# Moving a step's exponential behind its value products in a masked attention layer

## The chip, the cores and the metric

The kernel runs on one core of one Trainium2 chip. The metric is the device time of one execution in microseconds, taken as the median of several runs. A core has five engines that work side by side, each through its own queue of instructions in program order: TensorE (PE in the profile; its weight loads are shown apart as PEld), VectorE (DVE), ScalarE (ACT), GpSimd (POOL) and SyncE (SP, which here only issues transfers). They wait for each other through semaphores. TensorE's products land in PSUM, which the program divides into eight banks.

## The reference, cut to what matters

One graph-attention layer with a residual: x is 8 frames of 2048 rows by 256 channels, adj a 2048 x 2048 mask that all frames share, 8 heads of 32 channels.

```python
qkv = jnp.einsum('fnc,ck->fnk', x, w_qkv)
q, k, v = jnp.split(qkv, 3, axis=-1)
# ... reshaped to (F, N, H, D), H = 8, D = 32
scores = jnp.einsum('fnhd,fmhd->fhnm', q, k) / jnp.sqrt(jnp.asarray(D, x.dtype))
mask = (adj > 0)[None, None, :, :]
scores = jnp.where(mask, scores, jnp.asarray(-1000000000.0, x.dtype))
attn = jax.nn.softmax(scores, axis=-1)
t = jnp.einsum('fhnm,fmhd->fnhd', attn, v).reshape(F, N, C)
x = _layernorm(x + t, ln1_g, ln1_b)
h = jax.nn.relu(jnp.einsum('fnc,cd->fnd', x, w1) + b1)
f_out = jnp.einsum('fnd,dc->fnc', h, w2) + b2
x = _layernorm(x + f_out, ln2_g, ln2_b)
# ... and around the layer: x = _layernorm(x_in + layer(x_in))
```

## The kernel before

The attention is cut into **items** (f, qc, g, mb): frame f, a chunk qc of 512 queries, a group g of four heads, and a block mb of 128 keys. There are 8 x 4 x 2 x 16 = 1024 items. The sixteen items with the same (f, qc, g) form a **group**; there are 64 groups. One item is one **step** of the main loop.

A step computes the scores of the item two ahead (LEAD = 2), and the value products of its own item. `scores` makes four products, one for each head, into two PSUM pairs; VectorE adds the mask to them and writes them to SBUF, and ScalarE takes the exponential of all 128 x 2048 elements in place.

```python
def scores(item):
    f, qc, g, mb = item
    pt = PT[item] = pp.tile([P, 4, CH], F32, name="p")     # pp has 10 buffers
    ps2 = [score_pair() for _ in range(2)]                 # 3 pairs of banks, in turn

    for half in (1, 0):
        for j in range(2):
            r = D * (2 * half + j)
            nc.tensor.matmul(ps2[half][:, j, :], KT[...][r:r + D, ...],
                             QT[f, qc, g][r:r + D, :], start=True, stop=True)
    for half, ps in enumerate(ps2):
        nc.vector.tensor_tensor(pt[:, 2 * half:2 * half + 2, :], ps,
                                MK[f, qc][:, mb, None, :].to_broadcast([P, 2, CH]), ALU.add)
    nc.scalar.activation(pt, pt, AF.Exp, scale=1.0 / math.sqrt(D))

LAST = MB - 1

def values(item):
    f, qc, g, mb = item
    grp = (f, qc, g)
    if mb == 0:
        i = state["side"]
        O[grp] = ps_x[i].tile([P, CH], F32, name=f"x{i}")
    for h in range(4):
        r = D * h
        nc.tensor.matmul(O[grp][r:r + D, :], V[...][:, mb % TPC, r:r + D], PT[item][:, h, :],
                         start=(mb == 0), stop=(mb == LAST))
    if mb == LAST:
        OT[grp] = op.tile([P, CH], F32, name=f"oT{g}")
        nc.scalar.copy(OT[grp], O.pop(grp))
```

Six of the eight PSUM banks serve the scores. The two others, ps_x, change roles from group to group: one gathers the value products of the running group, and the other is the only bank for everything else (projections, transposes, the layer's dense part), which is called **fill** here. At a group's end the roles are swapped, so the bank that fill gets next is the one that the finished group's values are still in, until ScalarE has copied them out to oT.

```python
def bank(dt=F32):
    shape = [P, CH] if dt == F32 else [P, 2, CH]
    if state["side"] is not None:
        i = 1 - state["side"]
        return ps_x[i].tile(shape, dt, name=f"x{i}")
    # ... (only the opening, before the main loop)

def channels(pool, name, xT, k0):          # fill: queries and keys
    ps = bank()
    for a in range(2):
        nc.tensor.matmul(ps, wqkv[:, a, k0:k0 + P], xT[:, a, :], start=(a == 0), stop=(a == 1))
    t = pool.tile([P, CH], F32, name=name)
    nc.scalar.copy(t, ps)
    return t
# project(): channels() for the keys, then the values' projection, each after a "yield BANK"
# tail(), second dense product, fill too:
for jj in range(0, TPC, 2):
    yield BANK
    ps = bank()
    for j in range(jj, jj + 2):
        for d in range(2):
            nc.tensor.matmul(ps[:, (j - jj) * C:(j - jj + 1) * C], hT[:, d, j * P:(j + 1) * P], w2s[:, d, :], ...)
    nc.vector.tensor_tensor(z[:, jj:jj + 2, :], ps.rearrange(...), z[:, jj:jj + 2, :], ALU.add)
```

The main loop puts at most one piece of fill (`advance(t, 1)`) ahead of a step's scores, and none in a group's first step:

```python
for t, (f, qc, g, mb) in enumerate(items):
    if mb == 0 and t:
        state["side"] = 1 - state["side"]
    # ... (what fill is to start)
    if mb:
        advance(t, 1)
    if t + LEAD < len(items):
        # ... (brings a projection forward if its V is still missing)
        scores(items[t + LEAD])
    values(items[t])
    add_up(items[t])          # sums for the denominators: GpSimd adds and adding transfers
    if mb == LAST:
        start(t + SUM, denominator(f, qc, g), t)
```

Of the kernel before, what the change touches and what calls it, by code (L numbers as in the profile page):

```python
# [14 lines left out]
AF = mybir.ActivationFunctionType  # L15
# [5 lines left out]
D = 32  # L21
# [32 lines left out]
def fast_path(ctx, tc, cst, x, adj, out, RS):  # L54
    nc = tc.nc
# [24 lines left out]
    def score_pair():  # L80
        i = state["pair"]
        state["pair"] = (i + 1) % 3
        return ps_s[i].tile([P, 2, CH], F32, name=f"s{i}")
# [45 lines left out]
    def mask_blocks(qc, mc, cv):  # L129
        for half in range(2):  # L130
            yield BANK
            ps = bank(BF16)
            for r in range(2):
                for j in range(TPC):
                    rr = 2 * half + r
                    nc.tensor.transpose(ps[:, r, j * P:(j + 1) * P], cv[:, j, rr * P:(rr + 1) * P], identb)
            nc.vector.tensor_tensor(MK[0, qc][:, mc * TPC + 2 * half:mc * TPC + 2 * half + 2, :], ps,
                                    cst["ones"][:, 0:1, None].to_broadcast([P, 2, CH]), ALU.min, saturate=False)
        if mc == NCK - 1:
            nc.sync.dma_start(MD[qc], words(MK[0, qc]))  # L140

    def load_mask(f, qc):
        MK[f, qc] = mkp.tile([P, MB, CH], F8, name="mask")
        nc.sync.dma_start(words(MK[f, qc]), MD[qc])
# [5 lines left out]
    def queries(f, c, xT):  # L150
        for g in range(2):
            yield BANK
            QT[f, c, g] = channels(qp, "qT", xT, g * P)

    def turn_rows(xc, xT):
# [3 lines that stand above are left out]
            for j in range(TPC):  # L159
                nc.tensor.transpose(ps[:, j * P:(j + 1) * P], xc[:, j, a * P:(a + 1) * P], ident)  # L160
            nc.scalar.copy(xT[:, a, :], ps)
# [32 lines left out]
    def project(f, c, g, xT=None):  # L194
        if xT is None:
            xT = yield from reload(f, c)
            while len(KT) < (2 * f + g) * NCK + c:
                yield 1
        yield BANK
        KT[f, c, g] = channels(kp, "kT", xT, C + g * P)  # L200
        yield BANK
        ps = bank()
        for j in range(TPC):
            for a in range(2):
                nc.tensor.matmul(ps[:, j * P:(j + 1) * P], xT[:, a, j * P:(j + 1) * P],  # L205
                                 wqkv[:, a, 2 * C + g * P:2 * C + (g + 1) * P], start=(a == 0), stop=(a == 1))
        v = vp.tile([P, TPC, P], F32, name="v")
        nc.scalar.copy(v, ps.rearrange("p (j c) -> p j c", c=P))
        V[f, c, g] = v
        give(xT)  # L210


    PT, O, OT, RC = {}, {}, {}, {}

    def scores(item):
        f, qc, g, mb = item
        pt = PT[item] = pp.tile([P, 4, CH], F32, name="p")
        ps2 = [score_pair() for _ in range(2)]
# [4 lines that stand above are left out]
                nc.tensor.matmul(ps2[half][:, j, :], KT[f, mb // TPC, g][r:r + D, (mb % TPC) * P:(mb % TPC + 1) * P],  # L223
                                 QT[f, qc, g][r:r + D, :], start=True, stop=True)
        for half, ps in enumerate(ps2):
            nc.vector.tensor_tensor(pt[:, 2 * half:2 * half + 2, :], ps,  # L226
                                    MK[f, qc][:, mb, None, :].to_broadcast([P, 2, CH]), ALU.add)
        nc.scalar.activation(pt, pt, AF.Exp, scale=1.0 / math.sqrt(D))  # L228

    LAST = MB - 1  # L230

# [8 lines that stand above are left out]
            nc.tensor.matmul(O[grp][r:r + D, :], V[f, mb // TPC, g][:, mb % TPC, r:r + D], PT[item][:, h, :],  # L240
# [4 lines that stand above are left out]
# [8 lines left out]
    def add_up(item):  # L253
        f, qc, g, mb = item
        for chain in MOVED:
            if mb in chain[1:]:
                nc.gpsimd.dma_start(PT[f, qc, g, chain[0]], PT.pop(item), accum_op=ALU.add)  # L257
        if mb in POOLED[1:]:
            first = PT[f, qc, g, POOLED[0]]
            nc.gpsimd.tensor_tensor(first, first, PT.pop(item), ALU.add)  # L260
# [119 lines left out]
    def start(t, gen, due):  # L380
        fill.append([t, gen, 1, due])
        fill.sort(key=lambda e: e[3])
# [24 lines left out]
    def mask_ahead(qc):  # L407
        for mc in range(NCK):
            yield from turn_mask(qc, mc)

    items = [(f, qc, g, mb) for f in range(F) for qc in range(NCK) for g in range(2) for mb in range(MB)]
    LEAD = 2
# [6 lines left out]
    def begin():  # L419
        flat = [pp.tile([P, 4, CH], F32, name="p").rearrange("p a q -> p (a q)") for _ in range(NCK + NCK // 2)]  # L420
        cols = [t.bitcast(I32).rearrange("p (j m) -> p j m", m=CH) for t in flat[:NCK]]
        cv = [t[:, i * 2 * CH:(i + 1) * 2 * CH].bitcast(BF16).rearrange("p (j m) -> p j m", m=CH)
              for t in flat[NCK:] for i in range(2)]
        rows = [pp.tile([P, 4, CH], F32, name="p") for _ in range(NCK)]
        for c in range(NCK):
            xc = rows[c][:, 0:2, :].rearrange("p a (b c) -> p (a b) c", c=C)
            nc.sync.dma_start(xc, x[0, c * CH:(c + 1) * CH, :].rearrange("(j p) c -> p j c", p=P))
            nc.sync.dma_start(cols[c], adj[0:CH, c * CH:(c + 1) * CH].rearrange("(j p) m -> p j m", p=P))
        MK[0, 0] = mkp.tile([P, MB, CH], F8, name="mask")
        for c in range(NCK):  # L430
            nc.vector.tensor_scalar(cv[c], cols[c], 0.0, MASKED, op0=ALU.is_le, op1=ALU.mult)
            xT = rows[c][:, 2:4, :]
            yield from turn_rows(rows[c][:, 0:2, :].rearrange("p a (b c) -> p (a b) c", c=C), xT)
            nc.sync.dma_start(XD[0][c], xT)
            XT[0, c] = xT
            if c == 0:
                yield from queries(0, 0, xT)
            yield from project(0, c, 0, xT)
            yield from mask_blocks(0, c, cv[c])
        for k in range(LEAD):  # L440
            scores(items[k])
        for c in range(NCK):
            yield from project(0, c, 1, rows[c][:, 2:4, :])

# [5 lines left out]
    for _ in begin():  # L450
        pass
# [3 lines left out]
# [3 lines that stand above are left out]
        if f == 0 and g == 0 and mb == 0 and qc + 1 < NCK:  # L458
            start(t, mask_ahead(qc + 1), t + 28)
        if g == 1 and mb == 0 and (f or qc == NCK - 1) and (f + 1 < F or qc + 1 < NCK):  # L460
            load_mask(f + (qc + 1) // NCK, (qc + 1) % NCK)
        if f + 1 < F:
            for what, *which in NEXT.get((2 * qc + g, mb), []):
                due = t + MB // 2 if what is turn else items.index((f + 1, 0, which[1], which[0] * TPC)) - LEAD - 1
                start(t, what(f + 1, *which), due)
# [3 lines that stand above are left out]
            nf, _, ng, nmb = items[t + LEAD]  # L469
            t0 = t  # L470
            while (nf, nmb // TPC, ng) not in V:
                advance(t0, 1)
                t0 += 1
            scores(items[t + LEAD])
        values(items[t])
        add_up(items[t])
        if mb == LAST:
            start(t + SUM, denominator(f, qc, g), t)
    t = len(items)
# [128 lines left out]
def kernel(  # L608
# [56 lines left out]
    nc.gpsimd.memset(RS[:, 1], 1.0)  # L665

    fast_path(tc, cst, x, adj, out, RS)


# [49 lines left out]
```

## Time and profile before

| | |
|---|---|
| median of three runs | 3736.42 us (3731.55 to 3740.82) |
| profiled execution: span | 3732.1 us |
| mean granted TensorE clock | 0.977 |
| groups of 16 steps | 64, most of them 48 to 64 us from one copy of the values to the next |

The profile is read from top to bottom: first the busy time of each engine over the whole span, then the groups of instructions by source line, each with its total busy time, the mean duration of one, and the idle time of its engine just before it together with what ended that idle time. A short name such as "L244" is line 244 of the kernel before: L223 the score products, L226 the mask's addition, L228 the exponential, L240 the value products, L244 the copy of a group's values, L180 and L205 projections, L352 and L362 the two dense products, L136 the transposes of the mask in the first frame, L294 the denominators. The timeline lists instructions in order of their start; equal neighbours are merged, and one product shows as two records.

### The profile page before, as it was taken

How to read it: one execution, taken by the hardware profiler on the slowest of the kernel's cores; microseconds unless marked ns; L12 is line 12 of the kernel's file. 1: busy time of each engine (PE TensorE's matmuls, PEld its weight loads, DVE VectorE, ACT ScalarE, POOL GpSimd, SP SyncE). 2: the span in 40 equal slices, each digit the busy share in tenths (PEclk: the TensorE clock that was granted, in tenths of full speed). 3: DMA queues.
4: the chain of work that ended last, by engine and by line, in shares of the span. 5: the costliest groups of instructions: out<-in, count | busy, mean ns of one | idle time of the engine just before them, and what ended most of it. 6: DMA issues, size and time to landing. Idle time of an engine off the chain costs nothing. (4 is left out here: it accounts for less than half of the span.)

```text
span 3732.1 us, 53786 instructions
## 1 busy us (share of the span) xinstructions
PE 3241.8 (87%) x22020; PEld 1038.8 (28%) x22020; DVE 2760.8 (74%) x3203; ACT 2411.0 (65%) x1921; POOL 2599.1 (70%) x1363
## 2 busy tenths in 40 slices
PE   7877888899988899889998899889898889988884
PEld 4222223222322233222332223222232222322221
DVE  4777766877688766788677777777768877688883
ACT  3554555766667666766666776666666676677663
POOL 2555666777677775877667785777777777687775
PEclk9998999999999999999999999999999999999997
DMA  6766675776766775776766776676676676676664
GB/s 185 175 142 152 146 175 117 168 162 142 173 150 145 158 171 145 169 153 154 169 138 151 163 172 158 140 165 154 147 175 141 148 171 152 154 164 140 139 134 86
DMA packets 113774, 573.31 MB, mean 154 GB/s; under 512 B 10833, under 2 KB 27729, under 8 KB 60273
## 3 DMA queue, kind: packets, MB, share of 16 engines
q0 software_dynamic: 64848, 436.90, 58.1%
q1 hardware_dynamic: 47856, 131.61, 10.0%
q8 instruction: 174, 2.85, 0.3%
q10 hardware_dynamic: 816, 1.31, 0.1%
q14 instruction: 80, 0.65, 0.0%
HBM read 129.37 MB, written 37.75 MB: 45 GB/s over the span
## 5 line engine op out<-in xcount | busy, mean ns | idle before, releaser
L226 DVE TENSOR_TENSOR p<-s,mask 128x1024 f32<-128x1024 f32 x2048 | 2410.3, 1219 | 753.8 <-PE s L223 480.0
L228 ACT ACTIVATE p<-p 128x2048 f32<-128x2048 f32 x1024 | 1957.1, 1911 | 1232.9 <-DVE p L226 916.2
L260 POOL TENSOR_TENSOR p<-p 128x2048 f32<-128x2048 f32 x384 | 1835.9, 4810 | 653.6 <-ACT p L228 645.0
L223 PE MATMUL s<-qT,kT 32*128 32x512 f32 x8192 | 1193.2, 652 | 232.5 <-DVE p L226 231.0
L240 PE MATMUL x<-p,v 128*32 128x512 f32 x8192 | 1112.2, 616 | 0.0
L257 POOL DMA_DIRECT2D p<-p x384 | 382.7, 1018 | 351.2 <-ACT p L228 138.9
L223 PEld LDWEIGHTS s<-qT,kT 32*128 32x128 f32 x8192 | 325.3, 186 | 853.6 <-DVE p L226 695.6
L240 PEld LDWEIGHTS x<-p,v 128*32 128x32 f32 x8192 | 162.3, 108 | 795.2 <-issue 645.1
L180 PE MATMUL x<-in,wqkv 128*128 128x512 f32 x472 | 234.6, 620 | 23.1 <-ACT oT L244 10.2
L278 ACT ACTIVATE y<-y,nb,rs 128x256 f32<-128x256 f32 x384 | 224.9, 589 | 38.0 <-POOL nb L275 38.0
L294 PE MATMUL x<-p,ones 128*32 128x512 f32 x2048 | 246.3, 599 | 1.8 <-DVE y L364 0.9
L267 DVE BATCH_NORM_STATS2 st<-y 128x6 f32<-128x256 f32 x384 | 160.1, 417 | 27.1 <-DMA y<-in_x_dram 27.1
L362 PE MATMUL x<-w2s,hT 128*128 128x256 f32 x512 | 127.6, 392 | 45.7 <-ACT oT L244 42.3
L352 PE MATMUL x<-turned,w1s 128*128 128x512 f32 x256 | 128.8, 626 | 20.8 <-ACT hT L353 19.5
L180 PEld LDWEIGHTS x<-in,wqkv 128*128 128x128 f32 x472 | 80.3, 190 | 186.1 <-issue 69.8
L362 PEld LDWEIGHTS x<-w2s,hT 128*128 128x128 f32 x512 | 92.1, 190 | 112.0 <-ACT oT L244 68.6
L205 PE MATMUL x<-wqkv,in 128*128 128x128 f32 x896 | 114.9, 282 | 6.4 <-ACT kT L182 6.3
L205 PEld LDWEIGHTS x<-wqkv,in 128*128 128x128 f32 x896 | 104.2, 192 | 55.0 <-ACT kT L182 34.0
L364 DVE TENSOR_TENSOR y<-x,y 128x512 f32<-128x512 f32 x64 | 44.3, 692 | 94.9 <-PE x L362 94.7
L294 PEld LDWEIGHTS x<-p,ones 128*32 128x32 f32 x2048 | 64.0, 111 | 165.8 <-issue 129.7
L272 POOL TENSOR_TENSOR rs<-rs,mhalf 128x4 f32<-128x4 f32 x96 | 99.3, 1035 | 8.0
L341 PE MATMUL x<-ident,y 128*128 128x128 f32 x256 | 48.0, 299 | 54.5 <-ACT turned L342 38.8
(87 smaller groups left out, 1427.1 us busy)
## 6 DMA issues: line engine op xcount, KB each, us to landing
p<-p POOLq DMA_DIRECT2D x384, 1024.0 KB, 9.7
y<-in_x_dram POOLq DMA_DIRECT2D x64, 512.0 KB, 6.1
in<-xd SPq DMA_DIRECT2D x59, 512.0 KB, 8.0
mask<-md SPq DMA_DIRECT2D x28, 1024.0 KB, 6.6
out_dram<-y SPq DMA_DIRECT2D x32, 512.0 KB, 3.0
in<-in_x_dram SPq DMA_DIRECT2D x28, 512.0 KB, 6.9
xd<-in SPq DMA_DIRECT2D x28, 512.0 KB, 10.0
in<-in_adj_dram SPq DMA_DIRECT2D x24, 512.0 KB, 7.6
```

The source lines that it names most:

```text
L180: nc.tensor.matmul(ps, wqkv[:, a, k0:k0 + P], xT[:, a, :], start=(a == 0), stop=(a == 1))
L205: nc.tensor.matmul(ps[:, j * P:(j + 1) * P], xT[:, a, j * P:(j + 1) * P], wqkv[:, a, 2 * C + g * P:2 * C + (g + 1) * P], start=(a == 0), s ...
L223: nc.tensor.matmul(ps2[half][:, j, :], KT[f, mb // TPC, g][r:r + D, (mb % TPC) * P:(mb % TPC + 1) * P], QT[f, qc, g][r:r + D, :], start=Tr ...
L226: nc.vector.tensor_tensor(pt[:, 2 * half:2 * half + 2, :], ps, MK[f, qc][:, mb, None, :].to_broadcast([P, 2, CH]), ALU.add)
L228: nc.scalar.activation(pt, pt, AF.Exp, scale=1.0 / math.sqrt(D))
L240: nc.tensor.matmul(O[grp][r:r + D, :], V[f, mb // TPC, g][:, mb % TPC, r:r + D], PT[item][:, h, :], start=(mb == 0), stop=(mb == LAST))
L257: nc.gpsimd.dma_start(PT[f, qc, g, chain[0]], PT.pop(item), accum_op=ALU.add)
L260: nc.gpsimd.tensor_tensor(first, first, PT.pop(item), ALU.add)
L267: nc.vector.bn_stats(st, t[:, j, :])
L278: nc.scalar.activation(t[:, j, :], t[:, j, :], AF.Identity, bias=nb[:, j:j + 1], scale=rs[:, j:j + 1])
L294: nc.tensor.matmul(ps[r:r + D, :], cst["ones"], term[:, h, :], start=(n == 0), stop=(n == 3))
L362: nc.tensor.matmul(ps[:, (j - jj) * C:(j - jj + 1) * C], hT[:, d, j * P:(j + 1) * P], w2s[:, d, :], start=(d == 0), stop=(d == 1))
```

## The change

The exponential is taken out of `scores` and put behind `values` in the loop. In ScalarE's queue this alters the order in one place only: in a group's last step, the copy of the group's values now stands ahead of the exponential of the item two ahead, where it stood behind it. In the fifteen other steps `values` gives ScalarE nothing, so the queue is as it was. No instruction is added or taken away. The purpose is to hand the bank of a finished group to fill earlier.

```diff
@@ scores()
         for half, ps in enumerate(ps2):
             nc.vector.tensor_tensor(pt[:, 2 * half:2 * half + 2, :], ps,
                                     MK[f, qc][:, mb, None, :].to_broadcast([P, 2, CH]), ALU.add)
-        nc.scalar.activation(pt, pt, AF.Exp, scale=1.0 / math.sqrt(D))
+
+    def exponentials(item):
+        nc.scalar.activation(PT[item], PT[item], AF.Exp, scale=1.0 / math.sqrt(D))
@@ the opening, before the main loop
         for k in range(LEAD):
             scores(items[k])
+            exponentials(items[k])
@@ the main loop
             scores(items[t + LEAD])
         values(items[t])
+
+        if t + LEAD < len(items):
+            exponentials(items[t + LEAD])
         add_up(items[t])
         if mb == LAST:
             start(t + SUM, denominator(f, qc, g), t)
```

## The prediction

> **What bounds the kernel now.** I read the busy shares first, then the groups by line, then the copy L244 by its tile, then one group's end in the timeline. The page's first part:
>
> ```profile
> PE 3241.8 (87%) x22020; PEld 1038.8 (28%) x22020; DVE 2760.8 (74%) x3203; ACT 2411.0 (65%) x1921; POOL 2599.1 (70%) x1363
> ```
>
> TensorE is the fullest engine, but this is an average over two kinds of steps. Steps with a piece of fill take about 4 us and are paced by TensorE; steps without take about 2.5 us and are paced by VectorE, whose two mask additions need 2 x 1219 ns. So TensorE's idle time is worth looking at by its cause. Groups of TensorE's and ScalarE's instructions (busy, mean ns of one, then idle before and its releasers):
>
> ```profile
> L223 PE MATMUL s<-qT,kT 32*128 32x512 f32 x8192 | 1193.2, 652 | 232.5 <-DVE p L226 231.0
> ...
> L180 PE MATMUL x<-in,wqkv 128*128 128x512 f32 x472 | 234.6, 620 | 23.1 <-ACT oT L244 10.2 <-ACT turned L342 6.0 <-ACT qT L182 3.3
> ...
> L362 PE MATMUL x<-w2s,hT 128*128 128x256 f32 x512 | 127.6, 392 | 45.7 <-ACT oT L244 42.3 <-ACT hT L353 2.0 <-DVE y L364 0.9
> ...
> L136 PE MATMUL x<-identb,in 128*128 128x128 bf16 x192 | 16.2, 233 | 6.1 <-ACT oT L244 4.5 <-ACT hT L353 1.4
> ```
>
> Apart from the scores' wait for VectorE, the copy L244 is the largest single cause of idle time on TensorE. The answer for the tile oT gives the number of these waits:
>
> ```profile
> L244 ACT COPY oT<-x x64: 565/567/585, 123.2 to 3664.1; 128x512 f32<-128x512 f32 x64
> ...
>   PEld x L362: 68.6, 29
>   PE x L362: 42.3, 29
>   PEld x L180: 16.6, 7
>   PEld x L240: 13.2, 16
>   PE x L180: 10.2, 7
>   PE x L136: 4.5, 3
> ```
>
> 29 + 7 + 3 = 39 of the 64 group ends make TensorE wait for the copy, 42.3 + 10.2 + 4.5 = 57.0 us in all, 1.46 us at a time. The 25 others have no fill in the group's second step, so nobody asks for the bank. One of the 39 in the timeline (start, duration, then the instruction, idle before it in brackets):
>
> ```profile
> 1917.91 1.91 ACT L228 ACTIVATE p<-p 128x2048 f32<-128x2048 f32 x1 [1.55 <-issue]
> ...
> 1919.40 1.07 PE L240 MATMUL x<-p,v 128*32 128x512 f32 x8
> 1919.60 2.36 DVE L226 TENSOR_TENSOR p<-s,mask 128x1024 f32<-128x1024 f32 x2 [0.40 <-PE s L223]
> ...
> 1921.95 1.07 PE L240 MATMUL x<-p,v 128*32 128x512 f32 x8
> 1922.04 1.91 ACT L228 ACTIVATE p<-p 128x2048 f32<-128x2048 f32 x1 [2.22 <-DVE p L226]
> 1922.16 2.35 DVE L226 TENSOR_TENSOR p<-s,mask 128x1024 f32<-128x1024 f32 x2 [0.20 <-PE s L223]
> 1923.85 0.57 ACT L244 COPY oT<-x 128x512 f32<-128x512 f32 x1
> ...
> 1924.47 1.99 PE L362 MATMUL x<-w2s,hT 128*128 128x256 f32 x8 [1.46 <-ACT oT L244]
> 1924.88 1.91 ACT L228 ACTIVATE p<-p 128x2048 f32<-128x2048 f32 x1 [0.46 <-DVE p L226]
> ```
>
> The group's last value products end at 1919.40 + 1.07 = 1920.47. ScalarE has been idle since 1917.91 + 1.91 = 1919.82, but next in its queue is an exponential, whose scores VectorE finishes at 1921.96. So the copy, ready at 1920.5, starts at 1923.85 and ends at 1924.42. TensorE, done with the next item's values at 1923.02, starts the fill product at 1924.47.
>
> **What the Trainium skill says.** The page Perfetto Trace Analysis, section Tensor Engine Instruction, says that ScalarE, VectorE and GpSimd take their instructions strictly in order, while TensorE may pull a weight load ahead of products in flight. The trace agrees: the copy stood 3.4 us behind a waiting exponential; and weight loads overlap products (PEld 28% beside PE 87%), so I count only the waits of PE and not those of PEld. The page ScalarE: Activation LUTs, section What ACT_TABLE_LOAD costs, gives 186 ns + 0.833 ns an element for immediate scale and bias: 1892 ns for 2048 elements and 612 ns for 512, with successive ones overlapping by some 93 ns. The trace has 1911 and 567 ns, and an overlap of 1923.95 - 1923.85 = 0.10 us; I use the trace's. The page TensorE: Matmul & The Clock Gate, section HAM oscillation, warns of idle gaps above about 3.4 us, which cost TensorE its clock. 1.46 us is below that, and the trace shows no penalty: the L362 product after the wait took 1.99 us, and the one in the last step before it, which followed value products without a wait, also 1.99. So I add no gain from a better clock.
>
> **The change part by part.** Removed and added: no instruction, on any engine. Moved: in 64 of 1024 steps, the copy goes ahead of one exponential.
>
> *The copy.* It can start when the last value products are done, about 1920.52 in the example, and ends 0.57 us later at 1921.09. The bank is needed at 1923.02, so there are 1.9 us to spare and the whole wait of 1.46 us goes. The other 38 waits are the same to within 0.1 us (36 of 1.46, the three in the first frame around 1.5), because the same instructions stand in the same order. Sum: 57.0 us.
>
> *The exponential now behind the copy.* It can't start before VectorE's second addition, at 1922.04, 0.95 us after the copy's end, so it isn't delayed. In the timeline ScalarE's idle gap before this exponential is 0.92 us or more at each group end that has one to show, and most often 2.1: room for 0.57 us. Where the gap opens late and the exponential is pushed back by a few tenths, its values are wanted only two steps, about 5 us or more, after its scores. Cost: nothing.
>
> *What follows the earlier fill product.* In the example it would end at 1925.0. Its evacuation (L364, 0.69 us on VectorE) waited 1.99 us for it and moves with it; VectorE's additions for the item before end at 1924.5, so it is free. The next scores would go from 1926.40 to 1924.94; a pair of banks is free then, because VectorE has done the additions that empty it. So scores, additions and exponentials all move by 1.46 us. In the seven cases with a key projection (L180) the fill's own copy stands behind an exponential which VectorE holds: at the group end near 1859.79 it still starts at 1862.43 and ends at 1863.00, so the following fill (L205) starts at about 1863.06 instead of 1862.93. That loses 0.13 us x 7 = 0.9 us.
>
> Sum on the path: 57.0 - 0.9 = 56.1 us.
>
> *How much of it reaches the end.* After the group's end come several fill steps, in which TensorE sets the pace and VectorE waits for it (2.6 and 3.0 us idle ahead of instructions are common there), so a shift there is handed on to the VectorE-paced steps behind it, all of whose inputs are earlier by the same amount. What could hold part of it back are the ten p buffers that GpSimd and the adding transfers release: VectorE waited for such a transfer 25.8 us in 19 cases. If these grow slightly, some 2 us are lost. I take 54 us: 3736.4 - 54 = 3682 us, 1.4% less.
>
> **The rivals.** First, *ScalarE blocks on the copy*: if the copy stood waiting for late value products, or took room that the exponential needs, each group end would delay an exponential by up to 0.57 us, 64 x 0.57 = 36 us. Then 3682 + 36 = 3718, and 3773 if the gain failed too. Against it: value products follow the scores directly on TensorE and take 1.07 us, VectorE's two additions 2.36 us, so the copy's input is ready before the exponential's; and ScalarE is 65% busy. Second, *VectorE takes over the wait*: scores already wait 231 us for VectorE (333 times), and at the step after the group's last TensorE waited 0.41 us for it. If half of the gain turned into this wait, 3709; if all, 3736. Against it: in the example VectorE idles 1.99 us just behind the wait in question. It needs the earlier start as much as TensorE does. Third, *the gain is larger*: by the weight loads' waits for the copy, 68.6 + 16.6 + 13.2 = 98 us, one would get 3638, 2.6% less. Against it: these waits begin while TensorE is still busy with value products (2.37 us before the L362 load, of which 1.46 are idle for PE). Fourth, *buffers*: the 2 us that I allow for could be 15, if the GpSimd-heavy groups (about 47 of 56 us busy) are paced by it; 3695.
>
> **Range and chances.** The base has a spread of 9 us, and 56 us is nearly an upper bound, since only measured idle time is counted. A pass-through of 60 to 110% gives 3703 to 3675; with the spread of the runs I take 3669 to 3703. More than 2% would need 75 us, more than all waits for the copy: 4%. Slower by over 2% would need a new wait of 130 us: 1%. The rest, 95%, within 2%.
>
> **What would show it right or wrong.** Right: L244 vanishes as a releaser of L362, L180 and L136 (57 us to about nothing); TensorE's busy time stays at 3242 us within the clock's variation; ScalarE's idle time moves from ahead of L228 to ahead of L244, which then waits for L240; each of the 39 group ends has the fill product directly behind value products. Step two is wrong if exponentials at group ends start more than some tenths after VectorE's additions or L240 waits for L228. The pass-through is wrong if the scores' wait for L226 grows well beyond 231 us, or L226 waits much longer for transfers. The prediction would fail altogether if L244 stayed a releaser, that is, if the copy waited for something other than its place in the queue.

## The result and the profile after

| | before | after |
|---|---|---|
| median of four runs, us | 3733.99 | 3674.84 |
| lowest to highest | 3729.03 to 3740.82 | 3665.09 to 3686.12 |
| ratio, 95% interval | | 0.9841 (0.9808 to 0.9875) |
| profiled span, us | 3732.1 | 3671.6 |

The change saves 1.6%, inside the predicted range. Three line numbers of the part read here shift: the exponential is now L230, the value products are L242, the copy of a group's values is L246; the second dense product is L364. Groups of TensorE and ScalarE in the changed kernel (busy, mean ns; then idle time before, with its releasers):

```profile
L223 PE MATMUL s<-qT,kT 32*128 32x512 f32 x8192 | 1185.3, 648 | 243.3 <-DVE p L226 242.0 <-DVE mask L137 0.9
L242 PE MATMUL x<-p,v 128*32 128x512 f32 x8192 | 1105.3, 612 | 0.0
...
L180 PE MATMUL x<-in,wqkv 128*128 128x512 f32 x472 | 234.3, 619 | 15.8 <-ACT turned L344 6.0 <-ACT qT L182 3.6 <-DMA in<-xd 2.6
...
L364 PE MATMUL x<-w2s,hT 128*128 128x256 f32 x512 | 127.6, 392 | 3.1 <-ACT hT L355 1.8 <-DVE y L366 0.9
...
L136 PE MATMUL x<-identb,in 128*128 128x128 bf16 x192 | 15.2, 223 | 1.7 <-ACT hT L355 1.4
```

```profile
L246 ACT COPY oT<-x 128x512 f32<-128x512 f32 x64 | 37.1, 580 | 23.6 <-PE x L242 23.6
```

The copy is gone from the releasers of all three fill products. It now waits for the value products itself (23.6 us in all against 3.1), where ScalarE used to wait ahead of the exponential. The same group end as the prediction's, in the timeline:

```profile
1891.51 1.91 ACT L230 ACTIVATE p<-p 128x2048 f32<-128x2048 f32 x1 [1.56 <-issue]
...
1893.00 1.06 PE L242 MATMUL x<-p,v 128*32 128x512 f32 x8
1893.19 2.35 DVE L226 TENSOR_TENSOR p<-s,mask 128x1024 f32<-128x1024 f32 x2 [0.40 <-PE s L223]
1894.13 0.59 ACT L246 COPY oT<-x 128x512 f32<-128x512 f32 x1 [0.71 <-PE x L242]
...
1895.54 1.06 PE L242 MATMUL x<-p,v 128*32 128x512 f32 x8
1895.63 1.91 ACT L230 ACTIVATE p<-p 128x2048 f32<-128x2048 f32 x1 [0.91 <-DVE p L226]
...
1896.54 1.99 PE L364 MATMUL x<-w2s,hT 128*128 128x256 f32 x8
```

The copy starts 0.07 us after the end of the value products (1894.06), and is done at 1894.72, 0.91 us before the exponential behind it can start. That exponential starts 0.09 us after VectorE's second addition (1895.54), so it isn't late. In this trace the same holds at all 63 group ends that have an exponential behind the copy: it starts 0.08 us after the addition that it needs. And TensorE has no idle time ahead of the value products (L242). The fill product starts at 1896.54, right behind the next item's value products, without a wait.

Where the time went can be followed group by group. Measured from the tenth exponential of one group to the tenth of the next, the 39 stretches that hold a group end with a wait became shorter by 60.1 us together, 27 of them by 1.52 to 1.54 us each. The 24 others became shorter by 4.0 us together.

### The profile page after: what moved, and what is told of

The parts are those of the page before. It is cut to its first block, busy times and chain, and to the rows that moved or that the text cites. A ratio compares the mean times of both kernels' runs of the same rounds, so it can differ in the third digit from the quotient of the medians.

```text
span 3671.6 us, 53762 instructions
## 1 busy us (share of the span) xinstructions
PE 3225.8 (88%) x22020; PEld 1036.9 (28%) x22020; DVE 2761.3 (75%) x3203; ACT 2415.5 (66%) x1921; POOL 2600.5 (71%) x1363
## 5 line engine op out<-in xcount | busy, mean ns | idle before, releaser
L230 ACT ACTIVATE p<-p 128x2048 f32<-128x2048 f32 x1024 | 1957.1, 1911 | 1145.1 <-DVE p L226 825.4
L223 PE MATMUL s<-qT,kT 32*128 32x512 f32 x8192 | 1185.3, 648 | 243.3 <-DVE p L226 242.0
L242 PE MATMUL x<-p,v 128*32 128x512 f32 x8192 | 1105.3, 612 | 0.0
L242 PEld LDWEIGHTS x<-p,v 128*32 128x32 f32 x8192 | 161.9, 108 | 788.5 <-issue 601.2
L180 PE MATMUL x<-in,wqkv 128*128 128x512 f32 x472 | 234.3, 619 | 15.8 <-ACT turned L344 6.0
L354 PE MATMUL x<-turned,w1s 128*128 128x512 f32 x256 | 130.6, 633 | 21.1 <-ACT hT L355 19.7
L180 PEld LDWEIGHTS x<-in,wqkv 128*128 128x128 f32 x472 | 80.1, 189 | 178.0 <-issue 73.4
L364 PE MATMUL x<-w2s,hT 128*128 128x256 f32 x512 | 127.6, 392 | 3.1 <-ACT hT L355 1.8
L205 PE MATMUL x<-wqkv,in 128*128 128x128 f32 x896 | 114.9, 281 | 6.3 <-ACT kT L182 5.9
L205 PEld LDWEIGHTS x<-wqkv,in 128*128 128x128 f32 x896 | 104.2, 191 | 55.2 <-ACT kT L182 38.4
L364 PEld LDWEIGHTS x<-w2s,hT 128*128 128x128 f32 x512 | 92.0, 189 | 68.1 <-ACT hT L355 29.1
L343 PE MATMUL x<-ident,y 128*128 128x128 f32 x256 | 48.2, 300 | 54.0 <-ACT turned L344 38.8
L371 POOL TENSOR_TENSOR y<-y,be2r 128x1024 f32<-128x1024 f32 x32 | 93.2, 2912 | 0.2
```

What stands on the lines that cost most here:

```text
L230: nc.scalar.activation(PT[item], PT[item], AF.Exp, scale=1.0 / math.sqrt(D))
```

## The experiments

### Only the group ends without a wait, only those with one

The changed kernel, with the order chosen by group; `WAITING` lists the 39 groups at whose end the trace of before shows TensorE waiting for the copy. The first kernel measured below, with the new order at the 25 other ends only, has `not in` in place of `in`.

```diff
+        ahead = t // MB in WAITING
+        if t + LEAD < len(items) and not ahead:
+            exponentials(items[t + LEAD])
         values(items[t])
-        if t + LEAD < len(items):
+        if t + LEAD < len(items) and ahead:
             exponentials(items[t + LEAD])
```

> New order only at the 25 group ends where no fill asks for the bank in the group's second step; the 39 others keep the old order. The theory of the prediction (the gain is the bank handed over earlier to a fill that waits for it): no gain, ratio to the kernel before 1.000 within 0.2%, and TensorE's waits for the copy stay at 57 us. Rival (the gain comes from the order on ScalarE as such, or from a better clock in general): 25/64 of some 60 us, that is 23 us, ratio 0.994.

Measured: 3735.8 us, ratio 1.0002 (0.9988 to 1.0017).

> New order only at the 39 group ends where fill waits for the copy. The theory: the whole gain of the change, 39 x 1.53 = 60 us, ratio 0.984, waits for the copy gone. Rival (order as such): 39/64 of it, 36 us, ratio 0.990.

Measured: 3679.02 us, ratio 0.9844 (0.9829 to 0.9860). The answers for the tile oT, of the kernel with the 25 and then of the one with the 39 (who waited for the copy: us in total, times; PEld rows are weight loads, PE rows products):

```profile
  PE x L365: 42.6, 29
...
  PE x L180: 10.2, 7
  PE x L136: 4.0, 3
```

```profile
  PEld x L243: 44.6, 57
  ACT p L230: 3.2, 2
  DVE y L328: 1.4, 2
```

In the first, all of the old waits are there, and nothing is gained; in the second no product waits for the copy, and the whole gain is there. The rival, that the order as such or a better clock brings it, is out: 0.994 and 0.990 lie outside the two intervals, and the mean granted clock was 0.982 in the profiled run without a gain but 0.977, as before the change, in the one with it. The first kernel also settles two differences between the profiles of before and after. TensorE's busy time there is 3222.8 us, and the scores wait 244.5 us for VectorE, as in the changed kernel (3225.8 and 242.0; before: 3241.8 and 231.0), yet its time is that of before. So these two differences are neither part of the gain nor its price.

### The copy on VectorE, in the old order

```diff
-            nc.scalar.copy(OT[grp], O.pop(grp))
+            nc.vector.tensor_copy(OT[grp], O.pop(grp))
```

> Old order of the program, but VectorE copies a group's values instead of ScalarE. ScalarE's exponential isn't touched. The theory: the copy stands behind the two additions of the same step, which end at 1921.96 in the example, and takes about 0.65 us (estimated from the 692 ns of the addition of 128x512), so the bank is free at about 1922.7, before the 1923.02 at which TensorE asks: the 57 us of waits go. Against that the 25 VectorE-paced ends get 0.65 us longer each, 16 us: net about 44 us, ratio 0.988. Rival (what counts is an earlier or later exponential on ScalarE): no gain, ratio 1.00 or above, since VectorE only gets more work (42 us).

Measured: 3682.81 us, ratio 0.9860 (0.9842 to 0.9879). VectorE's group of the copy:

```profile
L244 DVE COPY oT<-x 128x512 f32<-128x512 f32 x64 | 43.6, 681 | 0.2 <-PE x L240 0.2
```

Nothing on ScalarE was put ahead of an exponential, VectorE got 43.6 us more to do, and most of the gain came all the same: no product waits for oT in this trace. What counts is when the bank comes free, whichever engine empties it. The median is 3.8 us above that of the kernel with the 39, and the intervals overlap. So a price of the 25 copies at VectorE-paced ends isn't resolved. The full price of 17 us (25 x 681 ns; I had expected 16) would mean a ratio of 0.989, outside the interval of this kernel.

### Useless copies ahead of the exponential

```diff
-            nc.scalar.copy(OT[grp], O.pop(grp))
+            for _ in range(4):                      # 6 in the other kernel
+                nc.scalar.copy(OT[grp], O[grp])
+            O.pop(grp)
```

The changed kernel itself ran beside them:

> The changed kernel once more, beside the next two on the same chip: ratio to the kernel before 0.984, within 0.3%.

Measured: 3673.78 us, ratio 0.9829 (0.9814 to 0.9845).

> The changed kernel, but the copy of a group's values is made four times in a row (three useless ones), all ahead of the exponential. In the group end near 1894 of the changed kernel the last copy would end at about 1896.1 (0.47 to 0.5 us for each further one), so the exponential there starts 0.4 us late, while the bank is still free before 1896.54, when TensorE has use for it. The theory (an exponential has about two steps of slack, only the bank counts): nothing is lost, ratio 0.984. Rival (ScalarE blocked ahead of the exponential costs the step): 64 x 0.4 = 26 us, ratio 0.991.

Measured: 3678.94 us, ratio 0.9839 (0.9821 to 0.9857): no difference from the changed kernel is resolved. The four copies are merged in the timeline:

```profile
1906.34 2.44 ACT L247 COPY oT<-x 128x512 f32<-128x512 f32 x4 [0.72 <-PE x L242]
1908.67 3.71 ACT L230 ACTIVATE p<-p 128x2048 f32<-128x2048 f32 x2
```

The exponential starts 2.33 us after the first copy's start, against 1.50 us in the changed kernel (1895.63 - 1894.13). It is 0.83 us late, twice what I had estimated. At the 39 ends with fill in the next group's second step no value product waits for it. At the 25 others some do:

```profile
L242 PE MATMUL x<-p,v 128*32 128x512 f32 x8192 | 1106.4, 612 | 7.5 <-ACT p L230 7.1
```

These are 12 waits of 0.26 to 0.82 us, all at the 25 ends, where VectorE sets the pace and the next steps are short. At six of them the exponential started 1.39 us later behind the first copy than in the changed kernel, and five of these six waits were 0.81 to 0.82 us. So by my estimate only some 0.58 us of delay (1.39 - 0.81) are free there. The 7.1 us are of the size of the 5.2 us between the medians, which the intervals can't resolve. The rival's 26 us are out. For the change itself the rival is settled by its own trace: with a single copy no exponential starts late.

> As before with six copies in a row: the last ends at about 1897.0, the bank comes some 0.5 us late, and the exponential 1.3 us late. The theory: only the bank's lateness costs, 39 x 0.5 = 20 us, ratio 0.989 to 0.990, and TensorE's wait for the copy is back with about 0.5 us a time. Rival (the exponential's lateness counts): 64 x 1.3 = 83 us, ratio 1.006.

Measured: 3745.1 us, ratio 1.0027 (1.0012 to 1.0042). This lies between the two expectations. The groups of TensorE:

```profile
L242 PE MATMUL x<-p,v 128*32 128x512 f32 x8192 | 1107.6, 613 | 29.2 <-ACT p L230 28.6
...
L366 PE MATMUL x<-w2s,hT 128*128 128x256 f32 x512 | 127.6, 392 | 39.5 <-ACT oT L247 36.3 <-ACT hT L357 1.8 <-DVE y L368 0.9
```

With 7.8 us ahead of L180 and 5.4 ahead of L136 the bank costs 49.5 us at the 39 ends, at most of them 1.25 us. My estimate of 0.5 us was wrong because these copies, all to the same tile, follow each other by 0.62 us (the six take 3.67 us) and not by 0.47 to 0.5. Here the other theory is also right in part: TensorE waits for exponentials, 28.6 us in 21 cases. All 21 are at the 25 other ends. At the 39, most exponentials start 2.07 us late and no value product waits for them. Together the two waits make 78 us; the scores' wait for VectorE is 18 us less than in the changed kernel of this series (225.8 against 243.6), and some 60 us remain. The profiled spans differ by 67 us and the medians by 71 us (3745.1 against 3673.78), so 7 to 11 us are not accounted for. So the theory was wrong to give every exponential two steps of slack: at the ends with fill 2.07 us of delay are free, at those paced by VectorE often only some 0.58 us.

### No fill in a group's second step

The kernel before with its old order on ScalarE:

```diff
-        if mb:
+        if mb > 1 or mb and f == 0:
             advance(t, 1)
```

> The kernel before with its old order on ScalarE, but in frames 1 to 7 no fill is put into a group's second step; it comes in the third at the earliest. Nobody asks for the bank before the copy is done. The theory: the 33 waits in these frames vanish, 33 x 1.53 = 50 us, ratio 0.987, if the fill left out finds room in later steps; TensorE's waits for the copy fall to the six or so of frame 0 (9 us). Rival (the second step itself is a good place for fill, or fill is short of places): part of it is lost to steps paced by VectorE at the front and crowded fill later, ratio 0.990 to 1.00.

Measured: 3697.7 us, ratio 0.9893 (0.9876 to 0.9910), a gain of 40 us. The order on ScalarE is the old one, and the wait goes because nobody asks early: of 39 waits 5 are left. It gains less than the change. The scores of this kernel:

```profile
L223 PE MATMUL s<-qT,kT 32*128 32x512 f32 x8192 | 1190.6, 651 | 254.8 <-DVE p L226 252.7 <-DVE mask L137 0.9
```

Before it was 231.0 us; but in the kernel with the 25 ends this wait was 13.5 us longer than before without a cost, so it proves little. The transposes L341 wait 34.3 us for the normalization, where it was 15.6 (and 24.7 instead of 38.8 us for a copy), and adding transfers hold VectorE up for 35.1 us instead of 25.8. How the missing 10 us divide between these was not taken apart.

### The exponential behind the next step's fill too

The same reading of the trace points to more. The copies with which ScalarE empties the fill bank stand behind waiting exponentials in other steps too, not only at group ends. In the changed kernel (the bank's next user is the second transposes, L160):

```profile
1797.63 0.66 PE L160 MATMUL x<-ident,in 128*128 128x128 f32 x4
1798.27 1.14 PE L223 MATMUL s<-qT,kT 32*128 32x512 f32 x8
1799.34 1.06 PE L242 MATMUL x<-p,v 128*32 128x512 f32 x8
1799.38 1.91 ACT L230 ACTIVATE p<-p 128x2048 f32<-128x2048 f32 x1 [0.88 <-DVE p L226]
...
1801.69 0.56 ACT L161 COPY in<-x 128x512 f32<-128x512 f32 x1
...
1802.31 0.65 PE L160 MATMUL x<-ident,in 128*128 128x128 f32 x4 [1.90 <-ACT in L161]
```

The edit to the changed kernel moves the exponential once more, to the next step, behind that step's fill and ahead of its scores:

```diff
+        if 0 < t <= len(items) - LEAD:
+            exponentials(items[t + LEAD - 1])
         if t + LEAD < len(items):
             # ...
             scores(items[t + LEAD])
         values(items[t])
-        if t + LEAD < len(items):
-            exponentials(items[t + LEAD])
```

> The change taken one step further: a step's exponential goes behind the next step's fill as well, just ahead of the next scores. Now the copies that empty fill's bank stand ahead of the exponential too. The theory (a copy that stands behind an exponential waiting for VectorE holds up the bank): TensorE's waits for the copies L161, L344, L355, L182 in the changed kernel (39 + 39 + 20 + 10 us) shrink, up to some 100 us more, 3575 to 3640 us, ratio to before 0.957 to 0.975. Rival (the exponential gets late: it waits behind the fill's copies and the normalizations, and value products then wait for it): the gain is eaten up, 3675 or more, and TensorE waits for the exponential ahead of L242, or GpSimd falls behind.

Measured: 3558.6 us, ratio to before 0.9535 (0.9513 to 0.9556): another 3.1% below the changed kernel. The same place in its timeline:

```profile
1744.09 0.66 PE L160 MATMUL x<-ident,in 128*128 128x128 f32 x4
1744.88 1.14 PE L223 MATMUL s<-qT,kT 32*128 32x512 f32 x8
...
1745.51 0.56 ACT L161 COPY in<-x 128x512 f32<-128x512 f32 x1
1745.95 1.06 PE L242 MATMUL x<-p,v 128*32 128x512 f32 x8
1746.00 1.91 ACT L230 ACTIVATE p<-p 128x2048 f32<-128x2048 f32 x1
1746.95 0.66 PE L160 MATMUL x<-ident,in 128*128 128x128 f32 x4
```

The copy ends at 1746.07, ahead of the exponential, and the transposes follow the value products without a wait. TensorE's idle time behind ScalarE's copies falls from 131 us in the changed kernel (L160 39.2, L343 38.8, L354 20.6, L303 16.8, L180 9.6, L205 5.9) to 3 us, and the profiled span falls by 125.6 us. The gain is above what I expected; I had left L303's and L205's waits (22.7 us) out of the sum. Value products don't wait for the exponentials here:

```profile
L242 PE MATMUL x<-p,v 128*32 128x512 f32 x8192 | 1108.6, 614 | 0.0
```

VectorE's waits for an adding transfer grew from 24.2 to 38.4 us, and the scores' wait for VectorE from 242.0 to 252.4 us. Whether these two belong together wasn't tested.

## Why the prediction was right

**What bounds the kernel, and how much there was to gain**: right. Counting TensorE's idle time behind the copy, and not that of the weight loads, gave 57.0 us; the 98 us of the third rival were not there.

**The copy**: right in mechanism, slightly small in size. Predicted were 1.9 us between the end of the copy and the need for the bank, and 1.46 us gained a time. The trace shows 1896.54 - 1894.72 = 1.82 us to spare, and 1.53 us gained. The 0.07 us more is the overlap: without a wait, the fill product starts a little before the modelled end of the products ahead of it (1895.54 + 1.06 = 1896.60), while the idle time of 1.46 us was counted from that end. 39 x 1.53 = 59.7 us.

**The exponential behind the copy**: right, 0.91 us to spare against 0.95 predicted in the example, and no exponential late at any group end. The reserve behind it was overrated. The prediction counted on two steps, about 5 us, between an exponential's scores and its values; with four copies 12 late ones were waited for, and at the ends paced by VectorE often only some 0.58 us are free. That is enough for the few tenths of a microsecond that the prediction spoke of, and the change needed none of it.

**What follows**: scores, additions and exponentials moved by the same amount, as predicted; VectorE's wait for the fill product fell from 94.7 to 51.3 us. The predicted loss of 0.13 us at the seven key projections is there at six of them: from the start of L180 to that of the L205 behind it 3.98 us passed before, and 4.10 us after, of which 0.05 us are a wait for the copy of the keys. At the seventh, in the first frame, nothing changed. That is 0.7 us in all, of 0.9 predicted.

**How much reaches the end**: all of it, not the 54 of 56 us that I took. Waits for adding transfers stayed at 24.2 us (25.8 before), so the 2 us allowed for them weren't lost. That and 39 times 0.07 us make most of the 5 us by which the gain of 59.2 us exceeds the predicted 54. The other 2.4 us between 3682 and 3675 come from the base: its median of four runs is 3733.99, not the 3736.42 that the prediction started from.

**The rivals**: ScalarE blocking is out, since no exponential started late; VectorE taking the wait over by the kernel with only the 39 ends (full gain) and by the one with only the 25 (the same higher VectorE wait, no gain). Buffers took no visible part in this change: the waits for adding transfers didn't grow.

Wrong in the list of signs was that TensorE's busy time would stay: it fell by 16 us (mean granted clock 0.977 before, 0.980 after). The kernel with the 25 ends has the same low figure and no gain, so this was a poor sign to choose.

## What to carry to other kernels

In an in-order queue, an instruction that is ready waits for the one ahead that isn't; so put what frees a scarce buffer ahead of what waits longer for its input and is wanted later. To size such a change, add up the idle time of the engine that sets the pace, by releaser, and check in one example of the timeline when the input is ready, when the result is wanted, and what the instruction put back can bear. The last can differ between steps of one loop, as the late exponentials showed. When it works in one place, look for the same pattern elsewhere: here it was worth twice as much in the steps that the change hadn't touched.

## What the runs showed of the hardware

ScalarE's copy of 128x512 from PSUM took mostly 567 ns where it started before the instruction ahead of it had ended, and 586 ns after idle time. Two ScalarE instructions on different tiles overlap by some 0.10 us in the timeline, but repeated copies to one tile started 0.62 us apart with 0.586 us each, without any overlap. VectorE's copy of the same values took 681 ns.
